# Features times W_a ahead of the aggregation sums, sums in pairs of 64 columns, and 4 KB runs for row 0's second sweep

## Chip, cores and metric

The kernel runs on one core of one Trainium2 chip. The metric is the device time of one execution in microseconds; lower is better. Before the change it is 345.31 us, the median of three runs.

## What is computed

Two graph layers over N = 4096 nodes with D = 64 features, and one dense adjacency matrix `adj` (4096 x 4096, float32, 64 MB, about 1% nonzero):

```python
# layer 0
h = relu(layernorm(x))
for k in range(2):                                  # two hops
    agg = adj @ h
    h = tanh(concatenate([agg, h], axis=1) @ W[k])  # W[k] is 128 x 64
x = x + h
# layer 1
h = relu(layernorm(x))
support = h @ weight                                # 64 x 64
mask = (adj != 0)
rank = cumsum(mask, axis=1); deg = rank[:, -1:]
k = minimum(deg, 100)
pos = rank - (deg - k)
w = mask * where(pos > 0, 0.5 ** (k - pos), 0)
x = x + (w @ support + bias)
```

W[k] has an upper half W_a, for the aggregate, and a lower half W_b, for the node's own features, so a hop is tanh(agg @ W_a + h @ W_b). Layer 1 needs, for each nonzero of a row, how many nonzeros come after it.

## The kernel before

**Tiling.** The adjacency lies transposed in DRAM, cut into 32 blocks of 128 source nodes (`NB`) by 4 "rows" of 1024 target nodes (`NCH`, `CW`). The host's layout, `adjA`, has 16 tiles of 1 MB for each row. A tile of rows 1 to 3 is two blocks by 1024 columns, 8 KB in a run for each partition. A tile of row 0, a "quad", is four blocks by 512 columns. TensorE multiplies features (stationary, 128 nodes by 64 or 128 columns) with the adjacency (moving, 512 columns), so the sums stand transposed in PSUM: features on the partitions, target nodes along the free dimension. Two matmuls with 64 feature columns, one for each half of the 1024 target nodes, go to the two halves of the array's columns (`agg_pair`, L278 to L283): a "pair". A written float32 matmul shows as two recorded instructions.

**Features.** `hxs[q]` holds 8 blocks of nodes with 128 columns: in `[:, :, :D]` the layer norm's output h, in `[:, :, D:]` the features x1 after the first hop, once they are known. `pre1` holds h transposed (`features_T`, L297), later the node's own share h @ W_b (`own_share`, L219), later other things.

**First sweep** (`sweep1`, L464). All four rows go by, 16 tiles each. For every tile TensorE adds h's sums, and VectorE and ScalarE turn the tile into byte codes, which count the nonzeros of each column (`count_tile`, L256). The first step of that, "marking", is done by VectorE (L261), or for chosen tiles ahead of time by ScalarE (`mark_on_act`, L240, two passes of L245 and L246): `marks0` and `MARKS1` list which. When row I is finished, x1 of its 1024 nodes is known, and the later rows take the second hop's sums along for blocks below 8 I ("fused"): there one matmul of 128 columns takes h and x1 together into two banks of `acc[0]` (L606 to L611), and blocks above go in pairs into `acc[1]` (L613). Row 1 has 8 fused blocks, row 2 has 16, row 3 has 24.

**Row end** (`finish_row`, L420; for row 3 `finish_last`, L639). ScalarE copies h's sums from both accumulators into two tiles T and the second hop's share into the lower halves of `xs`; TensorE multiplies T with W_a (`x1_of`, L213, which calls `paired`); VectorE adds the own share; ScalarE takes tanh. Some tiles later `x1_and_share` (L340) transposes x1 back to nodes and multiplies with the second hop's W_b in the same matmuls, and the results are copied away (`take`, L354). These generators go on a list of `steps`, advanced once for each tile. Row 0 has its own end in two halves (`finish_first`, L358). After a row, `set_after` and then `settle` (L452) subtract the totals from that row's codes, 16 times in the first sweep, at odd tiles of rows 2 and 3.

**Buffers and queues.** Tiles are loaded from SP's queue in order, into 5 ring buffers of 1 MB and into areas where codes are not yet needed. A load waits on SP until every reader of the buffer is done, and all loads behind it wait as well. Temporaries (`tmp`) rotate over 5 buffers.

**Second sweep** (`sweep2`, L930). The 72 blocks that were not fused are loaded again, 512 KB each, and TensorE adds x1's sums with a pair for each (`hop`, L977). A small planner with a clock for each engine (`use`, `pe`) decides while the program is built which comes next: a hop, or a unit of layer 1 (`layer1`, L857), which multiplies weights, decoded from the codes by ScalarE (`convert`, L809) or VectorE (L801, L804), with layer 1's features. The instruction order is fixed by it; it is only a model of the engines. Blocks of rows 2, 3, 2, 1 and 0 come in that order; row 0's 24 blocks are last. For those the load reads, for each partition, two runs of 2 KB (L950 to L952). When a row's last hop is done, `finish_x2` (L678) takes the sums to layer 1's features: copy S, matmul with W_a (L696), sum and tanh y, residual, layer norm. 56 of the 128 units are held back until the hops are done (`n_late`), and the last 32 need row 0's features.

The matmul form of L869, TensorE's layer 1 work, uses float32r and is one recorded instruction of 512 columns. Before the first tile PE does nothing; VectorE makes the first features from x, and `wz`, the weights spread over zeros, is cleared on it (L163).

Of the kernel before, what the change touches and what calls it, by code (L numbers as in the profile page):

```python
# [19 lines left out]
P = 128  # L20
# [24 lines left out]
def gnn_kernel(  # L45
# [113 lines left out]

    warm = spool.tile([P, 1], F32, tag="warm", name="warm")  # L160
    nc.vector.memset(warm, 0.0)
    nc.scalar.activation(warm, warm, AF.Square)
    nc.vector.memset(wz, 0.0)  # L163
# [49 lines left out]
    def x1_of(po, I, terms, xs, sums):  # L213
        paired(po, terms)
        nc.vector.tensor_tensor(sums, po, flat(pre1[:, chunk(I), :]), op=ALU.add)
        for c in range(NC):
            nc.scalar.activation(xs[c][:D], sums[c * D : (c + 1) * D, :], AF.Tanh)

# [139 lines left out]
    def finish_first(acc, quads):  # L358
# [4 lines left out]
        def x1_half(c):  # L363
            S = tmp(name="S")
            nc.scalar.copy(S, low[c])
            yield
            nc.tensor.matmul(po[c * D : (c + 1) * D], w0, S, start=False, stop=True)
            xs[c] = tmp(name="x1T")
            nc.scalar.activation(xs[c][:D], po[c * D : (c + 1) * D], AF.Tanh)
            yield  # L370
            for h in range(2):
                pt = nodes(banks[h])
                for t in range(2):
                    nc.tensor.matmul(
                        pt[:, t, :, c, :], by_t(xs[c])[:D, h, t, :], xw[:D],
                        start=t == 0 and c == 0, stop=True, skip_group_check=True,
                    )
            for h in range(2):
                nc.scalar.copy(
                    as_nodes(hxs[0][:, :, D:])[:, 2 * h : 2 * h + 2, c], nodes(banks[h])[:, :, 0, c]  # L380
                )

        def hop1(b):
            for c in range(NC):
                nc.tensor.matmul(  # L385
                    G[c * D : (c + 1) * D, :], at(b)[:, D:], part_of(quads[c, b // 4], b),
# [33 lines left out]
    def finish_row(I, acc):  # L420
        T = [tmp(name="T") for _ in range(NC)]
        for c in range(NC):
            nc.scalar.copy(T[c][:D], acc[0][:D, c, :])
            nc.scalar.copy(T[c][D:], acc[1][c * D : (c + 1) * D])
        xs = [tmp(name="x1T") for _ in range(NC)]
        for c in range(NC):
            nc.scalar.copy(xs[c][D:], acc[0][D:, c, :])
        both = tmp([P, CW], U8, name="both")
        yield
        x1_of(one(name="po"), I, (lambda c: w0, lambda c: T[c]), xs, T[1])  # L430
# [6 lines left out]
        take(hxs[I][:, :, D:], banks, 0)  # L437
# [26 lines left out]
    def sweep1():  # L464
# [5 lines left out]
        EARLY = 9  # L470
# [33 lines left out]
        def counted(k):  # L504
# [10 lines left out]
        MARKS1 = (5, 7, EARLY, EARLY + 1, 14)  # L515
        marks0 = {1: 3, 3: 5, 7: 7, 9: 11, 11: 13, 13: 15}
        F, S = features_T, own_share
        at_step = {
            1: [(F, 3)], 2: [(S, 3)], 3: [(F, 2)], 4: [(F, 1)], 5: [(F, 0)], 6: [(S, 2)], 8: [(S, 1)],
        }  # L520
        to_count = [*range(8), *range(9, 16), 8]

        for k in range(2 * NQ):
# [29 lines left out]
            for b in (4 * q + n for n in (2, 3, 0, 1)):  # L553
# [6 lines left out]
            order_ = {  # L560
                0: (1, 1, 2), 1: (0, 1, 0), 2: ("n", 0),
            }.get(k, ("n", "n") if k == 7 else ("n",))
# [24 lines left out]
        for k in range(2 * NQ, len(units)):  # L587
# [16 lines left out]
            for r in (1, 0):  # L604
                g = b - 1 + r
                if fused(I, g):  # L606
                    for c in range(NC):
                        nc.tensor.matmul(  # L608
                            acc[0][:, c, :], at(g), a[:, r, c * C : (c + 1) * C],
                            start=g == (3 if I == 1 else CB * I - 1), stop=g == (4 if I == 1 else 0),  # L610
                        )  # L611
                else:
                    agg_pair(acc[1], at(g)[:, :D], a[:, r], g == NB - 1, g == CB * I)  # L613
# [3 lines left out]
            if j % HB in (MARKS1 if j < 2 * HB else (5, 8, 11, 14)):  # L617
                mark(j)
            if I > 1 and n % 2 == 1:
# [19 lines left out]
    def finish_last(acc):  # L639
# [5 lines left out]
        T, xs = ([tmp(name=n) for _ in range(NC)] for n in ("T", "x1T"))  # L645
        for c in range(NC):
            nc.scalar.copy(T[c][:D], acc[0][:D, c, :])
            nc.scalar.copy(T[c][D:], acc[1][c * D : (c + 1) * D])
        for c in range(NC):
            nc.scalar.copy(xs[c][D:], acc[0][D:, c, :])  # L650
        use("ACT", 3.4, 0.2)
        yield
        x1_of(one(name="po"), I, (lambda c: w0, lambda c: T[c]), xs, T[1])
        use("ACT", 1.1, use("DVE", 0.7, use("PE", 0.9) + 0.2) + 0.1)
# [3 lines left out]
        take(hxs[I][:, :, D:], banks, 0)  # L658
# [271 lines left out]
    def sweep2(acc):  # L930
# [14 lines left out]
        def load(k, r, a, t):  # L945
# [31 lines left out]
        def hop(n):  # L977
# [3 lines left out]
            k, r, a, landed = tiles[n]  # L981
            agg_pair(accs[I], at(b)[:, D:], a, (I, b) == firsts[I], (I, b) == lasts[I])
            consumed(k, r, a, pe(0.86, False, landed) + 0.2)
            if n in (1, 3, 5):
                next(last, None)
            if (I, b) in ((0, 2 * CB - 1), (0, 3 * CB - 1)):
                space(place([P, CW], F32R, f"hx{b // CB}", "weights"), clock["PE"] + 0.2)
            for v in ends:
                if v - 10 <= n < v and state["fetch"]:
# [3 lines left out]
            if (I, b) == lasts[I]:  # L993
                gen = finish_x2(I, accs[I])
                chain.append((next(gen), gen))

# [17 lines left out]
        while n < total or state["done"] < len(units) or chain or outs:  # L1014
# [10 lines left out]
            while n + hops < min(total, len(tiles)) and tiles[n + hops][3] <= clock["PE"] + 0.1 + 0.86 * hops:  # L1025
                hops += 1
            if state["wide"]:
# [10 lines left out]
            elif go == 2:  # L1038
                hop(n)
                n += 1  # L1040
            else:
                later = [x[0] for x in chain[:1]]
                if n < total:
                    later.append(tiles[n][3])
# [44 lines left out]
```

## Time and profile before

| | us |
|---|---|
| runs | 344.79, 345.31, 347.46 |
| the profiled execution | 345.83 |
| its span, first to last instruction | 343.2 |
| PE busy / VectorE busy / ScalarE busy / GpSimd busy | 328.2 / 279.9 / 200.9 / 23.6 |
| DMA | 108.44 MB, 316 GB/s over the span |

The stages, from the chain of waits: the first features and cold start to 19.6 us; row 0 to 52.86; row 1 to 96.91; row 2 to 142.78; row 3 to 193.65; hops of rows 3 and 2 to 224; hops of rows 1 and 0 among layer 1's units to 302; the hand-over from the last hop to row 0's features to 316.8; the last 32 units and the output to 343.2.

How to read the views. A group's line gives the line of code, engine, operation, the tiles written and read, shapes and count, then busy time, mean of one, and the idle time just before with what ended it. "PE" is a matmul and "PEld" the load of its stationary operand, which runs beside other matmuls. Shares of busy time are averages: a stage tells what is worth something, not the span. The duration of one matmul contains its way through the array, so the cost of many in a row is read from their starts.

### The profile page before, as it was taken

To read this page: it belongs to the slowest core of one execution; us is meant where nothing else is said; L and a number is where in the kernel's file an instruction comes from. 1 tells how busy PE (TensorE), PEld (TensorE's weight loads), DVE (VectorE), ACT (ScalarE), POOL (GpSimd) and SP (SyncE) were. 2 spreads that over 40 slices of the span, in tenths; PEclk is the share of its full clock that TensorE was granted. 3 is DMA by queue.
4 is the path that set the end of the run, shared out by engine and by line. 5 is a ranking of instruction groups with operands and counts; after the bars stand their busy time and mean duration, and the time that the engine had idled before them with its cause. 6 is when DMAs were issued, how large, how long until landed. Compare 5 with 4: busy or idle time off the path is not lost.

```text
span 343.2 us, 3881 instructions
## 1 busy us (share of the span) xinstructions
PE 328.2 (96%) x1360; PEld 155.2 (45%) x1360; DVE 279.9 (82%) x439; ACT 200.9 (59%) x210; POOL 23.6 (7%) x21
## 2 busy tenths in 40 slices
PE   1899999999999999999999999999999999998995
PEld 0344433333344444344444343343454656367785
DVE  4899999998589999899999395688266799989953
ACT  2296782594466551474342434137378989979980
POOL 2340000000000000000000000422003000003000
PEclk9999999999999999999999999999999999999999
DMA  8999999999999999966988999999998958600012
GB/s 267 420 425 417 420 422 421 421 422 420 422 422 416 379 379 352 356 235 236 376 327 298 298 369 411 395 409 411 406 364 281 333 132 248 203 1 0 2 50 73
DMA packets 25474, 108.44 MB, mean 316 GB/s; under 512 B 2416, under 2 KB 3824, under 8 KB 17392
## 3 DMA queue, kind: packets, MB, share of 16 engines
q1 hardware_dynamic: 25456, 108.21, 82.5%
q8 instruction: 10, 0.16, 0.2%
q14 instruction: 8, 0.07, 0.1%
HBM read 107.15 MB, written 1.05 MB: 315 GB/s over the span
## 4 chain that ended last, share of the span: by engine, by line
PE 81%; DMA 6%; DVE 6%; ACT 3%; issue 3%; SPq 1%; ACTq 0%; POOL 0%; DVEq 0%; POOLq 0%
PE acc L608 24%; PE acc L280 15%; PE acc_low L280 13%; PE accl L869 12%; PE acc L555 4%; DMA ring<-in_adjA_dram 4%; PE acc_low L555 3%; PE po L211 2%; PE pto L917 2%; PE acc L385 2%; ACT weights L809 2%; DMA pre<-in_x_dram 2%; PE pt L348 2%; DVE weights L804 1%; DVE bits L801 1%
## 5 line engine op out<-in xcount | busy, mean ns | idle before, releaser
L809 ACT ACTIVATE weights<-codes 128x1024 fp32r<-128x1024 uint8 x90 | 86.7, 1045 | 12.3 <-PE accl L869 9.7
L608 PE MATMUL acc<-ring,hx 128*128 128x512 f32 x160 | 69.6, 594 | 0.0
L280 PE MATMUL acc<-ring,hx 128*64 128x512 f32 x288 | 66.8, 599 | 0.8 <-DMA ring<-in_adjA_dram 0.8
L869 PE MATMUL accl<-weights,feat 128*128 128x512 f32 x254 | 63.4, 400 | 1.3 <-DVE feat L743 1.0
L869 PEld LDWEIGHTS accl<-weights,feat 128*128 128x128 f32 x254 | 45.9, 188 | 21.2 <-ACT weights L809 6.4
L608 PEld LDWEIGHTS acc<-ring,hx 128*128 128x128 f32 x160 | 30.2, 190 | 39.3 <-issue 38.5
L456 DVE TENSOR_TENSOR codes<-codes,after 128x2048 uint16<-128x2048 uint16 x32 | 38.3, 1219 | 0.1
L280 PEld LDWEIGHTS acc<-ring,hx 128*64 128x64 f32 x288 | 19.3, 136 | 39.8 <-issue 29.8
L261 DVE TENSOR_SCALAR mbuf<-ring 128x2048 uint8<-128x2048 f32 x30 | 36.7, 1222 | 0.1
L246 ACT ACTIVATE codes<-codes 128x2048 uint8<-128x2048 int8 x19 | 36.3, 1910 | 0.6
L254 DVE TENSOR_SCALAR cnt<-codes 128x1024 uint16<-128x1024 uint16 (+1 forms) x80 | 29.9, 373 | 2.7
L804 DVE TENSOR_SCALAR weights<-bits 128x1024 fp32r<-128x1024 f32 x37 | 26.6, 719 | 6.7 <-PE accl L869 3.1
L253 DVE TENSOR_TENSOR codes<-mbuf,cnt 128x1024 uint16<-128x1024 uint16 (+1 forms) x50 | 29.8, 596 | 1.8
L245 ACT ACTIVATE codes<-ring 128x2048 int8<-128x2048 f32 x8 | 15.3, 1913 | 26.5 <-DMA ring<-in_adjA_dram 26.5
L801 DVE TENSOR_SCALAR bits<-codes 128x1024 uint32<-128x1024 uint8 x37 | 25.6, 691 | 0.8
L280 PE MATMUL acc_low<-ring,hx 128*64 128x512 f32 x104 | 25.9, 597 | 0.0
L717 POOL TENSOR_TENSOR pre<-pre,wb 128x512 f32<-128x512 f32 x4 | 5.5, 1380 | 273.5 <-DVE xc L193 273.5
L245 ACT ACTIVATE codes<-codes 128x2048 int8<-128x2048 f32 x11 | 21.0, 1912 | 4.4 <-DMA codes<-in_adjA_dram 4.4
L280 PE MATMUL acc_low<-codes,hx 128*64 128x512 f32 x88 | 21.4, 594 | 0.0
L555 PE MATMUL acc_low<-ring,hx 128*64 128x512 f32 x40 | 13.0, 782 | 8.0 <-DVE hx L201 6.9
L261 DVE TENSOR_SCALAR mbuf<-codes 128x2048 uint8<-128x2048 f32 x15 | 18.3, 1221 | 0.5 <-DMA codes<-in_adjA_dram 0.5
L253 DVE TENSOR_TENSOR codes<-codes,cnt 128x1024 uint16<-128x1024 uint16 (+1 forms) x25 | 14.1, 563 | 5.4 <-ACT codes L246 4.0
(99 smaller groups left out, 282.7 us busy)
## 6 DMA issues: line engine op xcount, KB each, us to landing
ring<-in_adjA_dram SPq DMA_DIRECT2D x74, 512.0 KB, 7.9
ring<-in_adjA_dram SPq DMA_DIRECT2D x37, 1024.0 KB, 8.5
codes<-in_adjA_dram SPq DMA_DIRECT2D x26, 1024.0 KB, 17.8
pre<-in_x_dram SPq DMA_DIRECT2D x4, 256.0 KB, 7.4
xres<-in_x_dram SPq DMA_DIRECT2D x4, 256.0 KB, 7.9
out_dram<-o SPq DMA_DIRECT2D x3, 256.0 KB, 2.6
out_dram<-o SPq DMA_DIRECT2D x2, 128.0 KB, 2.2
wb<-in_weights_dram SPq DMA_DIRECT2D x1, 192.0 KB, 6.5
```

What stands on the lines that cost most here:

```text
L245: nc.scalar.activation(sign, tile_of(I, a), AF.Sign)
L246: nc.scalar.activation(m, sign, AF.Square, scale=float((FLAG - 1 + 0.25) ** 0.5))
L253: nc.vector.tensor_tensor(q, m, cnt, op=ALU.add)
L254: nc.vector.tensor_scalar(cnt, q, 0x7F7F, None, op0=ALU.bitwise_and)
L261: nc.vector.tensor_scalar(m, tile_of(I, a), 0.0, float(FLAG - 1), op0=ALU.not_equal, op1=ALU.mult)
L280: nc.tensor.matmul(acc[c * D : (c + 1) * D, :], src, a[:, c * C : (c + 1) * C], start=first, stop=last,)
L456: nc.vector.tensor_tensor(q, q, a[:, None, :].to_broadcast([P, 4, CW // 2]), op=ALU.subtract)
L555: nc.tensor.matmul(low0[c][h * D : (h + 1) * D, :], at(b)[:, :D], part_of(a, b), start=b >= NB - 2 if c == 0 else k == 8 and b > 1, stop=b ...
L608: nc.tensor.matmul(acc[0][:, c, :], at(g), a[:, r, c * C : (c + 1) * C], start=g == (3 if I == 1 else CB * I - 1), stop=g == (4 if I == 1 ...
L804: nc.vector.tensor_scalar(w, state["bits"].bitcast(F32), 2.0 ** (127 - LOW), None, op0=ALU.mult)
L809: nc.scalar.activation(w, q, AF.Exp, scale=LN2, bias=BIAS)
L869: nc.tensor.matmul(sums[g][:, c, :], feats[J][:, k, :], w[:, c * C : (c + 1) * C], start=first, stop=last,)
```

## The change

The second half of each `hxs` column range is now filled early with h @ W_a (`weighted`), so that the first hop's sums are adj @ (h W_a) and need no product behind them. The halves swap roles when a row ends: x1 is written over h in `[:, :, :D]`, and the hops and `hop1` read `[:, :, :D]`. Row 0's own sums still use h and W_a at the end. Fused blocks take two pairs, one for each half of the features, the second into one bank of `acc[0]`. `row_end` replaces the copies and `x1_of`. Three matmuls of cleared `wz` go first on PE. The lists of what is done at which tile of the first sweep (`at_step`, `order_`, `marks0`, `MARKS1`, `EARLY`, the settles) change: 17 tiles are marked on ScalarE where it was 19, and three of the 16 settles go to row 1. In the second sweep row 0's loads take two blocks by 512 columns, one run of 4 KB, and `hop` uses two such tiles at once, four matmuls, then gives both back; the planner's times for the row end change, and it waits for two tiles in row 0.

```diff
+    nc.vector.memset(wz, 0.0)
+    zeros = wz.rearrange("p c k a e -> p (c k a e)")
+    start = two(name="pw")
+    for _ in range(3):
+        nc.tensor.matmul(start, zeros[:, :P], zeros, start=True, stop=True)
...
-    def x1_of(po, I, terms, xs, sums):
-        paired(po, terms)
-        nc.vector.tensor_tensor(sums, po, flat(pre1[:, chunk(I), :]), op=ALU.add)
+    def row_end(I, acc, sums):
+
+        xs = [tmp(name="x1T") for _ in range(NC)]
+        for c in range(NC):
+            nc.scalar.copy(xs[c][D:], acc[0][c * D : (c + 1) * D, 0, :])
+        nc.vector.tensor_tensor(sums, acc[1], flat(pre1[:, chunk(I), :]), op=ALU.add)
         for c in range(NC):
             nc.scalar.activation(xs[c][:D], sums[c * D : (c + 1) * D, :], AF.Tanh)
+        return xs
+
+    def weighted(I):
+
+        v = by_t(flat(pre1[:, chunk(I), :]))
+        pt = (one if I % 2 else two)(name="pg")
+        for t in range(TC):
+            nc.tensor.matmul(
+                pt[:, t * P : (t + 1) * P].rearrange("p (c e) -> p c e", c=NC),
+                v[:, t // 2, t % 2, :], wz[:, :, 0, 0, :],
+                start=True, stop=True, skip_group_check=True,
+            )
+        nc.scalar.copy(
+            as_nodes(hxs[I][:, :, D:]), pt.rearrange("p (t c e) -> p t c e", t=TC, c=NC)
+        )
...
     def finish_row(I, acc):
-        T = [tmp(name="T") for _ in range(NC)]
-        for c in range(NC):
-            nc.scalar.copy(T[c][:D], acc[0][:D, c, :])
-            nc.scalar.copy(T[c][D:], acc[1][c * D : (c + 1) * D])
-        xs = [tmp(name="x1T") for _ in range(NC)]
-        for c in range(NC):
-            nc.scalar.copy(xs[c][D:], acc[0][D:, c, :])
+        xs = row_end(I, acc, tmp(name="T"))
         both = tmp([P, CW], U8, name="both")
         yield
-        x1_of(one(name="po"), I, (lambda c: w0, lambda c: T[c]), xs, T[1])
         tot = tmp([P, CW], BF16, name="tot")
         totals(I, both, tot)
...
-        EARLY = 9
+        EARLY = 7
...
-        MARKS1 = (5, 7, EARLY, EARLY + 1, 14)
-        marks0 = {1: 3, 3: 5, 7: 7, 9: 11, 11: 13, 13: 15}
-        F, S = features_T, own_share
-        at_step = {
-            1: [(F, 3)], 2: [(S, 3)], 3: [(F, 2)], 4: [(F, 1)], 5: [(F, 0)], 6: [(S, 2)], 8: [(S, 1)],
-        }
+        MARKS1 = (6, 9, 12, 15)
+        marks0 = {1: 2, 2: 4, 7: 8, 10: 13, 11: 15}
+        F, G, S = features_T, weighted, own_share
+        at_step = {1: [(F, 3), (F, 2)], 2: [(G, 3), (G, 2)], 4: [(S, 2)], 5: [(F, 0)], 6: [(G, 0)], 7: [(F, 1)], 8: [(G, 1)], 9: [(S, 3)], 10: [(S, 1)]}
...
-            order_ = {
-                0: (1, 1, 2), 1: (0, 1, 0), 2: ("n", 0),
-            }.get(k, ("n", "n") if k == 7 else ("n",))
+            order_ = {0: (1, 2), 1: (1, 'n', 1), 2: (0,), 3: (0, 0)}.get(k, ("n", "n") if k == 7 else ("n",))
...
+                last = n == HB - 1 and r == 0
+                agg_pair(acc[1], at(g)[:, D:], a[:, r], g == NB - 1, last)
                 if fused(I, g):
-                    for c in range(NC):
-                        nc.tensor.matmul(
-                            acc[0][:, c, :], at(g), a[:, r, c * C : (c + 1) * C],
-                            start=g == (3 if I == 1 else CB * I - 1), stop=g == (4 if I == 1 else 0),
-                        )
-                else:
-                    agg_pair(acc[1], at(g)[:, :D], a[:, r], g == NB - 1, g == CB * I)
+                    agg_pair(
+                        acc[0][:, 0, :], at(g)[:, :D], a[:, r], g == (3 if I == 1 else CB * I - 1), last
+                    )
...
-            if j % HB in (MARKS1 if j < 2 * HB else (5, 8, 11, 14)):
+            if j % HB in (MARKS1 if j < 2 * HB else (7, 10, 11, 12)):
                 mark(j)
-            if I > 1 and n % 2 == 1:
+            if (I, n) in {(1, 6), (1, 10), (1, 15), (2, 1), (2, 5), (2, 7), (2, 9), (2, 11), (2, 13), (2, 15), (3, 1), (3, 3), (3, 5), (3, 7), (3, 9), (3, 13)}:
                 settle()
...
-                v = adjA[0].rearrange("(c q) p r (h i) -> q r h p c i", c=NC, h=2)
-                v = v[b // 4, b // 2 % 2, b % 2]
-                nc.sync.dma_start(a.rearrange("p (c i) -> p c i", c=NC), v)
+                nc.sync.dma_start(a, adjA[0, b % 2 * (NB // 4) + b // 4, :, b // 2 % 2, :])
...
+            if I:
+                agg_pair(accs[I], at(b)[:, :D], tiles[n][2], (I, b) == firsts[I], (I, b) == lasts[I])
+                pe(0.86, False, landed)
+            else:
+                for h in range(2):
+                    for c in range(NC):
+                        nc.tensor.matmul(
+                            accs[0][c * D : (c + 1) * D, :], at(b + h)[:, :D],
+                            tiles[n + c][2][:, h * C : (h + 1) * C],
+                            start=(0, b + h) == firsts[0], stop=(0, b + h) == lasts[0],
+                        )
+                pe(1.72, False, tiles[n + 1][3])
+            size = 1 if I else 2
+            for k, r, a, _ in tiles[n : n + size]:
+                consumed(k, r, a, clock["PE"] + 0.2)
```

`finish_last` changes like `finish_row`: `row_end` comes before its first `yield`, and the `yield` between the copies and the product is gone.

More of the change, by code (lines that the diff above doesn't have):

```diff
@@ L162, in gnn_kernel @@
     nc.scalar.activation(warm, warm, AF.Square)
-    nc.vector.memset(wz, 0.0)
     diff = tmp([P, P], name="diff")
@@ L379, in x1_half @@
                 nc.scalar.copy(
-                    as_nodes(hxs[0][:, :, D:])[:, 2 * h : 2 * h + 2, c], nodes(banks[h])[:, :, 0, c]
+                    as_nodes(hxs[0][:, :, :D])[:, 2 * h : 2 * h + 2, c], nodes(banks[h])[:, :, 0, c]
                 )
@@ L385, in hop1 @@
                 nc.tensor.matmul(
-                    G[c * D : (c + 1) * D, :], at(b)[:, D:], part_of(quads[c, b // 4], b),
+                    G[c * D : (c + 1) * D, :], at(b)[:, :D], part_of(quads[c, b // 4], b),
                     start=b == 3, stop=b == 4,
@@ L436, in finish_row @@
         counts = count_after(I, tot, [acc[0][:, c, :] for c in range(NC)])
-        take(hxs[I][:, :, D:], banks, 0)
+        take(hxs[I][:, :, :D], banks, 0)
         take(pre1[:, chunk(I), :], banks, 1)
@@ L644, in finish_last @@
         totals(I, bytes_[:, :CW], tot)
[L645 to L654, printed above, removed]
+        xs = row_end(I, acc, tmp(name="T"))
+        use("ACT", 1.3, use("DVE", 0.7, use("ACT", 1.3, 0.2)) + 0.1)
         yield
@@ L657, in finish_last @@
         counts = count_after(I, tot, [acc[0][:, c, :] for c in range(NC)])
-        take(hxs[I][:, :, D:], banks, 0)
+        take(hxs[I][:, :, :D], banks, 0)
         take(pre1[:, chunk(I), :], banks, 1)
@@ L980, in hop @@
                 accs[I] = two(name="acc1") if I == 1 else plow.tile([P, C], F32, tag="low", name="acc1")
-            k, r, a, landed = tiles[n]
-            agg_pair(accs[I], at(b)[:, D:], a, (I, b) == firsts[I], (I, b) == lasts[I])
-            consumed(k, r, a, pe(0.86, False, landed) + 0.2)
+            landed = tiles[n][3]
+            if I:
[13 more added lines that the diff above has]
+                consumed(k, r, a, clock["PE"] + 0.2)
             if n in (1, 3, 5):
                 next(last, None)
+            b += size - 1
             if (I, b) in ((0, 2 * CB - 1), (0, 3 * CB - 1)):
@@ L988, in hop @@
             for v in ends:
-                if v - 10 <= n < v and state["fetch"]:
+                if v - 10 <= n + size - 1 < v and state["fetch"]:
                     residual(blocks[v][0])
@@ L995, in hop @@
                 chain.append((next(gen), gen))
+            return size
         def run_chain():
@@ L1026, in sweep2 @@
                 hops += 1
+            if hops == 1 and not blocks[n][0]:
+                hops = 0
             if state["wide"]:
@@ L1038, in sweep2 @@
             elif go == 2:
-                hop(n)
-                n += 1
+                n += hop(n)
             else:
@@ L1043, in sweep2 @@
                 if n < total:
-                    later.append(tiles[n][3])
+                    later.append(tiles[min(n + (not blocks[n][0]), len(tiles) - 1)][3])
                 i = state["done"]
```

## Prediction

> **What bounds the kernel now.** I read the chain of waits first. In it TensorE has 81% of the span, and the biggest terms are matmul lines, all of adjacency times features:
>
> ```profile
> PE 81%; DMA 6%; DVE 6%; ACT 3%; issue 3%; SPq 1%; ACTq 0%; POOL 0%; DVEq 0%; POOLq 0%
> PE acc L608 24%; PE acc L280 15%; PE acc_low L280 13%; PE accl L869 12%; PE acc L555 4%; DMA ring<-in_adjA_dram 4%; PE acc_low L555 3%; PE po L211 2%; PE pto L917 2%; PE acc L385 2%; ACT weights L809 2%; DMA pre<-in_x_dram 2%; PE pt L348 2%; DVE weights L804 1%; DVE bits L801 1%
> ```
>
> Then busy time by stage, with stages cut where the chain changes row. Columns: busy PE, weight loads, VectorE, ScalarE and GpSimd with instruction counts, granted clock, DMA share, GB/s:
>
> ```profile
> 19.60:52.86 33.26, 33.26 (x194) 13.57 (x192) 30.79 (x67) 26.10 (x22) 2.93 (x3) 1.00 1.01 420
> 52.86:96.91 44.05, 44.05 (x174) 16.59 (x170) 38.01 (x58) 24.14 (x22) 0.00 (x0) 1.00 1.01 421
> 96.91:142.78 45.87, 45.87 (x151) 19.35 (x150) 43.82 (x59) 22.06 (x22) 0.00 (x0) 1.00 0.96 382
> 142.78:193.65 50.87, 50.87 (x144) 22.45 (x144) 46.53 (x62) 21.32 (x19) 0.00 (x0) 1.00 0.82 300
> 193.65:224.00 30.35, 29.51 (x140) 11.58 (x142) 19.61 (x25) 11.33 (x19) 3.83 (x2) 1.00 1.00 381
> 224.00:302.00 78.00, 77.82 (x336) 38.01 (x332) 58.50 (x86) 60.60 (x67) 7.15 (x4) 1.00 0.88 302
> ```
>
> The reader is to see that PE is busy for every microsecond of rows 0 to 3 (19.6 to 193.65) and, but for about 1 us, after that until 302. VectorE has 31 to 47 us in these stages, a little under PE. DMA is full to about 110 us, but PE is behind it: in the waits, PE itself waited for a ring tile 0.8 us in all after 200, and that was at 219 to 224. So a microsecond of PE work removed or added in the first sweep is a microsecond, unless a second engine catches up.
>
> Third, the chain in order of time gives PE's prices (start, us, what; a written fp32 matmul is two recorded ones):
>
> ```profile
> 52.86 2.14 PE acc_low L280 x9
> ...
> 113.25 27.66 PE acc L608 x64
> 140.91 1.87 PE acc_low L280 x8
> 142.78 1.23 PE po L211 x3
> ...
> 144.44 3.43 PE acc_low L280 x15
> ```
>
> A pair of 64-column matmuls (x4) costs 0.86 (3.43 / 4 = 0.858); one fused block (x4 of L608) costs 27.66 / 16 = 1.73, which is two pairs. The first stretch of pairs behind a fused one takes 1.87, not 1.72.
>
> **What the Trainium skill says.** (1) "TensorE: Matmul & The Clock Gate", Part 1: an idle TensorE runs at half clock until it has been busy for a window of about 3.4 us, and falls back after an idle window. The trace agrees, from the start of the timeline (start, us, what):
>
> ```profile
> 6.87 3.68 PE L555 MATMUL acc_low<-ring,hx 128*64 128x512 f32 x8 [6.87 <-DVE hx L201]
> ...
> 11.72 3.63 PE L555 MATMUL acc_low<-ring,hx 128*64 128x512 f32 x8 [1.17 <-DMA ring<-in_adjA_dram]
> ...
> 16.05 1.90 PE L555 MATMUL acc_low<-ring,hx 128*64 128x512 f32 x8
> ```
>
> The first two tiles take 3.68 and 3.63 for 8 instructions, the third 1.90. (The granted-clock row reads 1.00 throughout; the durations decide.) (2) "TensorEngine Tiling (Array Packing)", Key Properties: a change of tiling mode drains the array. The trace agrees: 1.87 - 1.72 = 0.15 per change. (3) "DMA: Bandwidth & Descriptors", "Why small descriptors are slow (HBM only)": every packet has a fixed overhead. At 255 to 260 us, with row 0's 2 KB runs, the engines are fully busy at 329 GB/s, against 404 to 413 earlier with 4 KB runs.
>
> **The change part by part.** Negative is a gain.
>
> *Zeros first.* Three fp32 matmuls wait only for wz to be cleared (0.48 us, now first on VectorE, so ready near 1.3) and at half clock take about 3 x 1.71 = 5.1, ending near 6.5; the first real matmul starts at 6.87 when its features are there, so they lie in idle time. If the clock is up by then, tile 1, which cannot start before its data at 11.72, takes 1.90, not 3.63: -1.7. The idle time between tile 0 and tile 1 grows from 1.2 to 2.9 us, under the skill's window. The 0.76 us of waiting before the own share at 18.70 also goes, because that share moves to the ninth step: -0.8. Against this, row 3's and row 2's transposes now sit together after tile 1, and the second waits for features that VectorE writes near 14.5 (its order now puts them ahead of row 1's second sum; 15.68 before). The products that follow wait for ScalarE's two copies of 0.6, queued behind the two copies of the weights: about +0.3. Taken -2.2; bounds -2.5 and, with a cold clock and longer waits, +0.5.
>
> *Features times W_a.* Four times four matmuls of 128 columns. The nearest row is the same form, py of L696: 1.14, plus 0.15 for the mode change, less one change where two stand together: 4 x 1.29 - 0.15 = +5.0. PE is full there, nothing hides them. ScalarE's four copies (0.63 each) replace other copies and find it 26 of 33 us busy.
>
> *Pairs in place of fused columns.* 48 fused blocks cost 7.06 + 7.06 + 27.66 + 41.40 = 83.2; as 96 pairs 96 x 0.858 = 82.4; four changes of mode behind them are 4 x 0.15. Together -1.4. Not shown before is a pair to one bank alternating with a pair to another. The nearest is row 0, where L385 follows L555 in another bank at 0.86 each; bounds -1.4 and +4.
>
> *Row ends.* W_a no longer follows the sums. In row 2, from 142.78 to the next transpose at 147.87 are 5.09, of which 3.43 are the next row's pairs: 1.66 for the two matmuls, because the second waits for ScalarE's copies. Rows 1 and 2: -3.3. The chain is now one copy pair (2 x 0.58) on ScalarE beside one addition (0.69) on VectorE, then two tanh (2 x 0.64): 2.6, beside three tiles (5.2) of the next row, so no wait. Queued behind the addition on VectorE is the next row's counting, and behind that the release of ring tiles; it stands earlier in that queue than before, and VectorE had finished counting row 2 at 140.4, ahead of PE's 142.78. In row 3 only two pairs (1.87) cover the 2.6: 1.65 - 0.8 = -0.85, and then the ring is late next (0.79 us of DMA waits at 219 to 224 already), so -0.5; bounds 0 and -1.65.
>
> *Moved marks and settles.* Two fewer tiles are marked on ScalarE (2 x 3.82 less) and two more on VectorE (2 x 1.22), three of sixteen settles (1.2 each) go from rows 2 and 3 to row 1. Row 1 had 6 us of VectorE time free (38.0 of 44.05, one wait of 3.95), which takes the 6.1 added there with nothing to spare; rows 2 and 3 have 3.7 less. Zero; if the cover fails, VectorE is late at row 1's end by 1 to 2 us, where the 2.6 us of slack hide it. Bounds -0.3 and +2.
>
> *Row 0's 4 KB runs, used in twos.* Each 512 KB tile takes about 1.28 (410 GB/s) and not 1.59 (329). SP's queue issues the same number of loads in the same order, and the residual loads stand at the same places. PE waited for none of these tiles, it had weights to work on. Zero; bounds -1 and +0.3 (the first tile of two is given back 0.86 later).
>
> *The hand-over at the end.* The chain from the last hop, VectorE and PE:
>
> ```profile
> 303.42 0.68 DVE L687 COPY S<-acc 128x512 f32<-128x512 f32 x1
> ...
> 304.16 1.21 PE L696 MATMUL py<-wz,S 128*128 128x128 f32 x8 [0.49 <-DVE S L687]
> ...
> 306.55 0.68 DVE L702 TENSOR_TENSOR y<-py,pre 128x512 f32<-128x512 f32 x1
> ```
>
> The last hop ends at 302.0. The copy S waits on VectorE until 303.42, the sum y until 306.55, both behind conversions and evictions; the features are ready at 316.6 (end of VectorE's L743). In the changed order S is on ScalarE, and that eviction comes before it: up to 1.5 sooner. Two units (2 x 0.465) move ahead of the last hop: up to +0.9. Taken -0.7, bounds -2.5 and +1.
>
> **Sum.** -2.2 + 5.0 - 1.4 - 3.3 - 0.5 - 0.7 = -3.1 (0 for the rest). The profiled execution took 345.83 (span 343.2 and 2.6 around it), 0.5 above the median of 345.31, within the runs' scatter. Forecast **342.7**, 0.8% under the median.
>
> **The rivals.** *A, as summed* (0.55): 342.7, own range 340.5 to 344.8. *B, the tail gives more* (0.20): the hand-over's full -2.5 and row 3's full -1.65 make -6.1, 339.8. For it: ScalarE and VectorE are both full at 280 to 305, so the position of one copy counts. Against it: the 24 units left to do in the hand-over are 11.2 us, and no weights can pass before the features. *C, the zeros do not do what they say* (0.12): the array is cold again, or still, at 11.72, and the start returns -0.3: about 344.6. For it: zeros fill 5.1 us, and a window that doesn't start with them can miss. *D, slower* (0.13): a 64-column pair alternating between two banks, with twice as many weight loads, loses its overlap. Its price is 96 pairs times the excess; it decides from 3.1 / 96 = 0.03 us per pair, and 0.07 makes it 349.4. Against it: weight loads of pairs take 137 ns of about 430, and row 0 alternates at 0.86.
>
> **How the numbers follow.** No change is taken as within 1% (341.9 to 348.8), about what runs between 344.79 and 347.46 can tell. Faster: 0.21 of A and 0.19 of B, 0.40. Slower: 0.08 of D and 0.02 of mishaps in A, 0.10. Same: 0.50. The range 339.0 to 347.0 leaves out most of D and the low end of B.
>
> **What would show it.** Zeros: tile 1 at 11.7 with 1.9, not 3.6. W_a: four groups of 8 at 1.1 before 45 us. Pairs: 0.86 in the fused rows, and 1.72 behind them. Row ends: pairs straight up to the transpose in rows 1 and 2; a gap under 1 us in row 3. So the row ends should come later by about 2.8 at 52.86, by 0.2 at 142.78 and earlier by about 2 at 193.65. 4 KB runs: 400 GB/s after 255 with PE's times unchanged. The forecast is wrong if PE shows waits inside rows 1 to 3, or if the last hop moves by 2 and the end does not.

## The result and the profile after

The change made the kernel slightly faster. The changed kernel takes 343.27 us (median of 21 runs, 341.91 to 345.75) against 345.20 for the kernel before in the same comparison (21 runs); the ratio is 0.9956, 95% interval 0.9938 to 0.9974. It was timed twice more beside the experiments: 0.991 (0.9878 to 0.9943) and 0.9927 (0.9899 to 0.9955). The forecast, 342.7 against 345.31, was a ratio of 0.9924. It lies below the first interval and inside the other two.

The profiled execution of the changed kernel takes 343.04, its span 341.3. Two further profiles of the same kernel, from the repeats, have spans of 341.4 and 340.0. The table shows the effect and how much one execution differs from another (us from the start of the span; "first unit" is the first layer-1 matmul):

| | before | after | repeat 1 | repeat 2 |
|---|---|---|---|---|
| row 0's end on PE | 52.86 | 55.60 | 56.79 | 55.59 |
| row 3's end | 193.65 | 191.85 | 193.04 | 191.84 |
| row 0's end to row 3's end | 140.79 | 136.25 | 136.25 | 136.25 |
| row 3's end to first unit | 31.09 | 31.89 | 30.86 | 30.68 |
| first unit | 224.74 | 223.74 | 223.90 | 222.52 |
| first unit to the end of the span | 118.5 | 117.6 | 117.5 | 117.5 |

The steps that the trace can hold to 0.1 us are the rows (4.5 gained) and the stretch behind the first unit (0.9 gained). The start and the stage before the first unit move by more than a microsecond between executions of one program.

The timeline of the start, of the changed kernel (start, duration, engine, line, operation; in brackets the wait before it and what ended it):

```profile
1.45 5.49 PE L164 MATMUL pw<-wz 128*128 128x512 f32 x6 [1.45 <-DVE warm L166]
6.87 2.04 PE L568 MATMUL acc_low<-ring,hx 128*64 128x512 f32 x8
11.49 1.94 PE L568 MATMUL acc_low<-ring,hx 128*64 128x512 f32 x8 [2.59 <-DMA ring<-in_adjA_dram]
```

Tile 1 (11.49) takes 1.94 where it took 3.63, behind a wait of 2.59. So far this is what the prediction said of the zeros; the experiments say something else.

Busy time by stage of the changed kernel, with stages cut at its own row ends (columns as in the prediction):

```profile
55.60:97.23 41.63, 41.63 (x198) 14.89 (x196) 39.91 (x62) 18.98 (x16) 0.00 (x0) 1.00 1.01 421
97.23:141.10 43.87, 43.87 (x213) 15.78 (x210) 42.60 (x60) 19.83 (x17) 0.00 (x0) 1.00 0.95 385
141.10:191.83 50.73, 50.73 (x244) 18.08 (x242) 43.95 (x61) 20.87 (x18) 0.00 (x0) 1.00 0.86 309
191.83:223.81 31.98, 29.88 (x139) 10.32 (x135) 21.30 (x26) 9.45 (x16) 3.83 (x2) 1.00 1.00 385
```

These stages end where a row's sums end. In the kernel before, the cuts at 96.91 and 142.78 lie two pairs of the next row later: row 1's sums ended at 95.04 and row 2's at 140.91.

```profile
87.98 7.06 PE acc L608 x16
95.04 1.87 PE acc_low L280 x8
```

Cut alike, rows 1, 2 and 3 were 42.18, 45.87 and 52.74 and are 41.63, 43.87 and 50.7. PE is still busy for all of them: no waits, and VectorE at 39.9 to 44.0 has not become the bound. In the stage behind row 3 (191.83 to 223.81), PE is busy for 29.88 of 31.98 and DMA for all of it. The first part of the chain in order of time shows why the rows are shorter, and where row 3 still waits:

```profile
75.77 0.86 PE acc L302 x4
76.63 0.86 PE acc_low L302 x4
...
141.10 5.15 PE acc_low L302 x24
146.25 2.08 PE pt L370 x16
...
191.87 0.58 ACT x1T L221
...
193.72 0.64 ACT x1T L224
194.41 1.92 PE pt L370 x14
```

Pairs to `acc` and `acc_low` alternate at 0.86 each. At the end of row 2 six pairs follow (5.15), then at once the transposes at 146.25: nothing of the old row end is left. In row 3 the chain leaves PE for ScalarE's four operations, 191.87 to 194.36.

The hand-over at the end:

```profile
301.66 0.59 ACT L685 COPY S<-acc 128x512 f32<-128x512 f32 x1 [0.99 <-PE acc L987]
...
315.35 1.86 PE L870 MATMUL accl<-weights,feat 128*128 128x512 f32 x7 [1.54 <-DVE feat L744]
```

The copy S now starts 0.1 after the last hop (301.56) instead of 1.4 after it. The hand-over, from the last hop to row 0's features in use, is 13.8 instead of 14.8; two more units stand ahead of the last hop.

### The profile page after: what moved, and what is told of

Same layout as the page of the kernel before. It is cut to its first block, busy times and chain, and to the rows that moved or that the text cites. A ratio compares the mean times of both kernels' runs of the same rounds, so it can differ in the third digit from the quotient of the medians.

```text
span 341.3 us, 4305 instructions
## 1 busy us (share of the span) xinstructions
PE 329.6 (97%) x1578; PEld 150.1 (44%) x1578; DVE 280.4 (82%) x439; ACT 190.5 (56%) x199; POOL 23.5 (7%) x21
## 3 DMA queue, kind: packets, MB, share of 16 engines
HBM read 107.15 MB, written 1.05 MB: 317 GB/s over the span
## 4 chain that ended last, share of the span: by engine, by line
PE 82%; DMA 12%; DVE 3%; ACT 1%; SPq 0%; issue 0%
PE acc_low L302 25%; PE acc L302 20%; PE accl L870 16%; PE acc L987 6%; DMA codes<-in_adjA_dram 5%; DMA ring<-in_adjA_dram 5%; PE acc L568 4%; PE pto L918 2%; PE acc L407 2%; DMA wb<-in_weights_dram 2%; PE pt L370 2%; PE py L697 1%; PE acc_low L568 1%; PE po L215 1%; PE pg L232 1%; PE pt L396 1%
## 5 line engine op out<-in xcount | busy, mean ns | idle before, releaser
L302 PE MATMUL acc<-ring,hx 128*64 128x512 f32 x352 | 86.3, 597 | 1.7 <-DMA ring<-in_adjA_dram 1.7
L302 PE MATMUL acc_low<-ring,hx 128*64 128x512 f32 x264 | 65.5, 593 | 0.0
L302 PEld LDWEIGHTS acc<-ring,hx 128*64 128x64 f32 x352 | 23.6, 136 | 52.5 <-issue 39.8
L302 PEld LDWEIGHTS acc_low<-ring,hx 128*64 128x64 f32 x264 | 19.0, 137 | 37.5 <-issue 37.4
L267 ACT ACTIVATE codes<-ring 128x2048 int8<-128x2048 f32 x10 | 19.1, 1908 | 27.7 <-DMA ring<-in_adjA_dram 27.6
L283 DVE TENSOR_SCALAR mbuf<-ring 128x2048 uint8<-128x2048 f32 x28 | 34.2, 1221 | 0.0
L268 ACT ACTIVATE codes<-codes 128x2048 uint8<-128x2048 int8 x17 | 32.5, 1910 | 0.5
L302 PE MATMUL acc_low<-codes,hx 128*64 128x512 f32 x120 | 27.8, 593 | 0.0
L987 PE MATMUL acc<-ring,hx 128*64 128x512 f32 x96 | 21.9, 598 | 0.0
L202 POOL TENSOR_TENSOR s<-s,half 128x8 f32<-128x8 f32 (+1 forms) x10 | 16.9, 1688 | 18.2 <-DVE s L201 18.2
L302 PEld LDWEIGHTS acc_low<-codes,hx 128*64 128x64 f32 x120 | 8.5, 137 | 17.0 <-issue 17.0
```

The lines of the kernel that those rows point to most:

```text
L267: nc.scalar.activation(sign, tile_of(I, a), AF.Sign)
L268: nc.scalar.activation(m, sign, AF.Square, scale=float((FLAG - 1 + 0.25) ** 0.5))
L283: nc.vector.tensor_scalar(m, tile_of(I, a), 0.0, float(FLAG - 1), op0=ALU.not_equal, op1=ALU.mult)
L302: nc.tensor.matmul(acc[c * D : (c + 1) * D, :], src, a[:, c * C : (c + 1) * C], start=first, stop=last,)
L987: nc.tensor.matmul(accs[0][c * D : (c + 1) * D, :], at(b + h)[:, :D], tiles[n + c][2][:, h * C : (h + 1) * C], start=(0, b + h) == firsts[ ...
```

## The experiments

The theory at the outset was the prediction's sum; in the first profile its terms up to row 3's end had about the forecast size. The questions were why a lead of 4.9 us in front of row 3's hops (they resume at 196.76 instead of 201.62) left 1.0 at the first unit, and whether the terms that came out right did so for the stated reason. Ratios are to the kernel before on the same chip. Runs e1 to e4 had no run of the changed kernel beside them; the later ones had.

### Without the zeros (e1, e7), and the zeros alone (e10)

e1 leaves out the three products:

```diff
-    zeros = wz.rearrange("p c k a e -> p (c k a e)")
-    start = two(name="pw")
-    for _ in range(3):
-        nc.tensor.matmul(start, zeros[:, :P], zeros, start=True, stop=True)
```

> The changed kernel without the three matmuls on zeros at the start. Theory (first-sweep time is kept, in part): tiles 0 and 1 take about 3.6 us each and not 2.0, the end of row 0 on PE comes 1 to 2 us later than 55.60, and the span grows by 0.5 to 1.5 us over 341.3, because the ring's loads after row 3 take up some of it. Rival (the zeros lie in idle time and tile 1 waits for data anyway): row 0 ends within 0.3 us of 55.60, span within 0.3.

Measured: 342.58 us, ratio 0.9929 (0.9904 to 0.9954); span 339.5, row 0's end at 54.55, 1.05 earlier than with the zeros. In that execution tile 1 had landed when tile 0 was done, and the clock came up in the middle of the two. e7 takes the zeros away as well, and moves row 3's transposes by one hop (next section):

> The changed kernel without its three products of zeros, and with the two transposes of row 3 after the third hop rather than the second. Theory (the zeros bring nothing, the hop's place brings 0.65 by returning ring slots sooner, and the two add up because the first loads of row 1's tiles are then the limit): ratio 0.986 to 0.991, first unit of layer 1 near 222 to 223. Rival (the zeros are worth 1 us or more in most executions, the profiled ones before were lucky): ratio 0.992 to 0.996, with tiles 0 and 1 at 3.6 each in the profile and row 0's end at 56.5 or later.

Measured: 342.10, ratio 0.9922 (0.9892 to 0.9951), against 0.991 (0.9878 to 0.9943) for the changed kernel beside it. The start of e7:

```profile
6.95 3.68 PE L564 MATMUL acc_low<-ring,hx 128*64 128x512 f32 x8 [6.95 <-DVE hx L201]
11.30 1.94 PE L564 MATMUL acc_low<-ring,hx 128*64 128x512 f32 x8 [0.67 <-DMA ring<-in_adjA_dram]
```

Tile 0 is cold, as before the change; tile 1 waits 0.67 and runs at full speed, without any zeros. Row 0's end is at 54.84. Both sides of the expectation fail: there is no gain over the changed kernel beside it, and the two tiles were not both cold. e1 fits neither side either: the theory wanted 0.5 to 1.5 lost and the rival no change within 0.3, and the span is 1.8 shorter.

e10 adds the zeros alone to the kernel before, with `wz` cleared ahead of them:

> The kernel before with only the three products of zeros added and wz cleared first. By the prediction's step: tile 0 and tile 1 at 1.9 to 2.2 instead of 3.7 and 3.6, row 0's end at about 51.2 (52.86 before), and the time 0.3 to 0.6% less. Rival (tile 1 waits for its data and the clock may have fallen back, so the start is won in some executions only, and what is won is waited for elsewhere): row 0's end between 51.5 and 53 and the time within 0.25% of the kernel before.

Measured: 345.41 us, ratio 0.9998 (0.9974 to 1.0023): the zeros alone bring nothing, within 0.9 us. PE and ScalarE at the start of e10:

```profile
7.35 1.94 PE L559 MATMUL acc_low<-ring,hx 128*64 128x512 f32 x8 [0.82 <-DVE hx L205]
...
11.31 1.94 PE L559 MATMUL acc_low<-ring,hx 128*64 128x512 f32 x8 [2.03 <-DMA ring<-in_adjA_dram]
...
17.12 0.63 ACT L198 ACTIVATE sq<-xc 128x512 f32<-128x512 f32 x1 [1.96 <-DVE xc L197]
...
17.66 0.60 ACT L310 COPY pre<-ph 128x512 f32<-128x512 f32 x1
...
18.31 1.08 PE L215 MATMUL po<-pre,wz 128*64 128x512 f32 x4 [1.91 <-ACT pre L310]
```

Here both tiles are warm, 3.4 us less of PE work, and row 0's end is at 52.47, only 0.4 earlier. The own share at 18.31 waits 1.91 instead of 0.76, because its operand is the copy `pre<-ph` on ScalarE at 17.66, which stands behind a layer-norm square that could not start before 17.12. That is what the rival said: the start of the kernel before was bound by the features there, not by PE.

What follows: a warm start is paid back at the next wait in the old order. In the new order tile 1 was warm without zeros in both executions that were profiled, and what the zeros take off tile 0 is waited for at tile 1: 2.59 in the changed kernel and 0.67 in e7, for a tile that starts at 11.49 and at 11.30. No run shows a gain from the zeros.

The clock's side of it shows in the changed kernel and in the other runs that have the zeros. Tile 1 took 1.94 in the changed kernel, e2, e4 and repeat 2, after waits of 2.6 to 2.8; 2.41, 2.66 and 2.82 in e5, repeat 1 and e8, after 2.6 to 2.9; and 3.42 in e3, after 2.67. The first two lines are from repeat 1, the third from e3:

```profile
11.83 2.66 PE L568 MATMUL acc_low<-ring,hx 128*64 128x512 f32 x8 [2.72 <-DMA ring<-in_adjA_dram]
14.21 2.98 PE L324 MATMUL ph<-ident,hx 128*64 128x128 f32 x32
...
11.89 3.42 PE L568 MATMUL acc_low<-ring,hx 128*64 128x512 f32 x8 [2.67 <-DMA ring<-in_adjA_dram]
```

Where the clock falls during tile 1, the transposes behind it are slow too (2.98 in repeat 1, 2.13 in the changed kernel), so e5, repeat 1 and e8 lost as much as e3. From the start of tile 1 to the end of these transposes it is 3.7 in the four executions that keep the clock, 5.2 in these three and 5.0 in e3. In repeat 1 the granted clock is 0.50 from 12.98 to 16.30. A lost clock costs 1.3 to 1.5 here, and row 0 ends at 56.4 to 57.1 instead of 55.6.

How often this happens can be counted, because the record has the mean granted clock of every execution. In the profiles that keep the clock it is 0.997 to 1.000, in those that lose it after the start 0.989 to 0.994. (A cold start is not counted: the kernel before has 1.000 with its two slow tiles.) Executions with 0.995 or less:

| | executions |
|---|---|
| kernel before | 3 of 78 |
| kernel before with zeros (e10) | 5 of 14 |
| changed kernel | 21 of 37 |
| changed kernel without zeros (e1, e7) | 1 of 17 |

In each of the three comparisons of the changed kernel, these executions have a median 1.1 to 1.9 us above that of the others. So on this record the zeros make it more likely that the clock is lost, and they may cost more than they bring. That is a count and not an experiment: the changed kernel with and without its zeros was not run side by side, its variants with the zeros go from 0 of 6 (e2) to 11 of 16 (e8), and where the clock fell is known for the profiled executions only.

The Trainium skill, "TensorE: Matmul & The Clock Gate", Part 1, says that the window of about 3.4 us is free-running, so that it depends on its phase when a kernel's clock changes. The waits above agree: nearly equal waits keep the clock in some executions and lose it in others, and the slow stretch of repeat 1 is 3.3 us long.

### Where the lead before the first unit went (e2, e3, e4, e8)

e2 moves row 3's transposes behind the third hop, so that they never wait for tanh and one ring slot is given back before them:

```diff
-            if n in (1, 3, 5):
+            if n in (2, 4):
```

> The changed kernel, with row 3's transposes of x1 after the third hop of the second sweep and not after the second. Theory (the ring's loads bound the stage to 224 us, and the third hop's ring slot comes back too late because it stands behind transposes that wait for tanh): the 0.36 us of waiting before the transposes goes, the third hop ends 2.5 us earlier, the first unit of layer 1 starts 0.5 to 1.3 us before 223.8, and the span falls by as much. Rival (the loads run at 410 GB/s throughout and nothing in the order of four hops moves them): first unit within 0.2 us of 223.8, span within 0.3 of 341.3.

Measured: 341.10 us, ratio 0.9884 (0.9864 to 0.9904); no wait ahead of the transposes, first unit 0.65 earlier than in the changed kernel. It was run again, beside the changed kernel:

> The changed kernel with row 3's transposes after the third hop, a second time. Theory (the ring's slots come back 0.86 us sooner to the loads that limit the stage from 200 to 224): first unit at 222.9 to 223.3, span 0.5 to 0.8 less than the changed kernel's beside it, time 0.1 to 0.4% less. Rival (the lower time of the first look came from the execution, not from the hop's place): first unit at 223.6 or later and times within 0.1%.

Measured: 343.91, ratio 0.9952 (0.9928 to 0.9976), against 0.9927 (0.9899 to 0.9955) for the changed kernel beside it. The first unit came at 224.41, in an execution that lost the clock at tile 1 and had row 0's end 1.6 later than in e2. The theory's gain is not there. The rival has its first unit, but not its 0.1%: the medians are 0.25% apart, with intervals that overlap. So the lower time of e2 is not shown to be a property of the hop's place. e1 and e7, which differ in that place alone, both have their first unit at 221.94. The same program in two comparisons gave 0.9884 and 0.9952, further apart than either interval. The clock goes with it: none of the six executions of e2 has a mean granted clock of 0.995 or less, but 11 of the 16 of e8. Those 11 have a median of 344.17, the other five 341.83, and e2 341.10.

e3 and e4 add the same 1.72 us of PE work, two pairs into an unused bank, in two places: ahead of the seventh hop of the stage, and in the middle of row 2.

```diff
+            if n == 6:          # e4: if k == 40, in the first sweep
+                pad = two(name="pad")
+                for _ in range(2):
+                    agg_pair(pad, at(b)[:, :D], tiles[n][2], True, True)
```

> The changed kernel with 1.72 us of extra PE work (two pairs into a spare bank, not used) before the seventh hop of the second sweep. Theory (PE is ahead of the ring there): PE's waits for the ring at 211 to 222, 1.7 us in all, shrink by it, the first unit of layer 1 still starts within 0.4 us of 223.8, the span stays within 0.4 of 341.3. Rival (PE is the bound in this stage too): everything behind it moves by 1.7.

> The changed kernel with the same 1.72 us of extra PE work in row 2 of the first sweep. Theory (the slots that start the second sweep's loads come back when PE has used the tiles, so this time is kept): row 3 ends 1.7 later, the first unit of layer 1 starts 1.0 to 1.7 later, and the span is 1.0 to 1.7 longer. Rival (the ring stage or the decoding behind it takes it up like that in the hops): first unit and span within 0.5 us of the changed kernel's.

Measured: e3 341.92, ratio 0.9925 (0.9898 to 0.9953); e4 344.10, ratio 0.9983 (0.9964 to 1.0002), on the same chip. PE's waits for the ring between 193 and 226, in the changed kernel and then in e3 (line, what it waited for, us in total, times, longest):

```profile
PE acc L302 <- DMA ring<-in_adjA_dram: 1.7, 8, 0.3
```

```profile
PE acc L302 <- DMA ring<-in_adjA_dram: 0.5, 1, 0.5
```

With 1.72 more work PE waits 1.2 less, and the first unit stays at 223.8, although row 0 had ended 1.1 later in this execution (the cold tile 1 above). Repeat 1, which ended row 0 as late and has no extra work, has it at 223.9. So in this stage PE runs ahead of the loads, and work put there is mostly hidden. In row 2 less is hidden: row 3's transposes came 1.76 later than in the first profile, but the first unit at 224.45 and the end of the span (342.0) only 0.7 later, between the 1.0 that the theory asked for and the rival's 0.5. The time is above e3's with disjoint intervals, by 0.6% or 2 us, which is more than was added. The lost clock does not explain it: the executions above 0.995 differ as much (341.57 and 343.74). PE work in the rows counts, work in this stage counts little; how much of a microsecond in the rows is kept, the profile and the times do not agree on.

What became of the 4.9 us: two hops of 0.86 were only moved, from ahead of row 3's transposes to behind them, so 3.1 are a real lead. By the first unit the first profile kept 1.0 of it, with 1.7 of waits for the ring. Repeat 2 resumed its hops at 196.74, with the same lead, and kept 2.2, with waits of 1.1; repeat 1 had a lead of 2.0 and kept 0.8. So the ring took about 1 to 2 us of the lead, and how much differs from one execution to the next. The difference between the first profile and repeat 2 begins on SP's queue: the residual load that stands between the last tile of the ring and the next took 1.65 us to issue from 194.70, and 0.55 from 194.34 in repeat 2. From 195 to 200 the DMA moved 301 GB/s in the one and 343 in the other, which at 410 GB/s is 0.5 us of transfer that isn't made up in a stage that is full. What held that issue up is open.

### Row 0's loads (e5)

e5 puts back the loads of two 2 KB runs, single hops, and (not shown) the two conditions by which the planner waits for tiles in twos:

```diff
-                nc.sync.dma_start(a, adjA[0, b % 2 * (NB // 4) + b // 4, :, b // 2 % 2, :])
+                v = adjA[0].rearrange("(c q) p r (h i) -> q r h p c i", c=NC, h=2)
+                v = v[b // 4, b // 2 % 2, b % 2]
+                nc.sync.dma_start(a.rearrange("p (c i) -> p c i", c=NC), v)
...
-            size = 1 if I else 2
+            size = 1
```

> The changed kernel with row 0's second-sweep loads as before: 2 KB runs, each tile used by itself. Theory (the 4 KB runs were hidden, PE had weights to work on): DMA share of 1.00 at about 329 GB/s in 255 to 260 comes back, PE has no wait there, and the time is within 0.3% of the changed kernel (under 1 us). Rival (they carry part of the gain: the ring's slots come back to the last hops earlier): slower by 1 us or more, with PE waits for a ring tile between 255 and 302.

Measured: 343.84, ratio 0.9969 (0.9946 to 0.9992), against 0.991 (0.9878 to 0.9943) beside it: the change without its 4 KB runs, used in twos, is 0.6% slower. From the first unit to the end of the span it takes 118.8; the eleven other profiles with the changed second sweep have 117.2 to 117.6. From 255 to 260 the DMA share is 0.96 at 335 GB/s, and 0.81 at 324 in the changed kernel. The stretch before the last hop of e5, and then of the changed kernel:

```profile
289.06 7.95 PE L302 MATMUL acc<-ring,hx 128*64 128x512 f32 x36
297.88 1.08 PE L302 MATMUL acc<-ring,hx 128*64 128x512 f32 x4 [0.87 <-DMA ring<-in_adjA_dram]
298.89 2.14 PE L870 MATMUL accl<-weights,feat 128*128 128x512 f32 x8
300.95 1.94 PE L302 MATMUL acc<-ring,hx 128*64 128x512 f32 x8
```

```profile
286.97 5.78 PE L870 MATMUL accl<-weights,feat 128*128 128x512 f32 x24
292.67 8.95 PE L987 MATMUL acc<-ring,hx 128*64 128x512 f32 x40
301.56 1.20 PE L870 MATMUL accl<-weights,feat 128*128 128x512 f32 x4
```

In e5 the ring is late for the hop at 297.88 (0.87), and the hops behind 255 come in seven stretches between units; in the changed kernel they come in five, the last of them ten pairs long. The last hop ends 79.4 after the first unit instead of 77.8. Of these 1.55, 0.87 is the wait; two stretches more are four changes between hops and units, 0.6 as an estimate from the prediction's 0.15 each. The hand-over behind it is 0.3 shorter, which leaves 1.2. The theory fails. The lower DMA share alone was no measure of it: PE waited for none of these tiles in the kernel before, but the changed kernel's PE with the old loads does. The shorter runs and the other order of hops were put back together, so their shares are not separated.

### The lists of the first sweep (e6, e9)

e6 takes all lists of the first sweep from the kernel before (`EARLY`, `MARKS1`, `marks0`, `order_`, the settles, and `at_step` with each new product one step after its features):

> The changed kernel with the lists of the kernel before: which row-0 and first-sweep tiles are marked early and on ScalarE, when settles come, and at which step of row 0 features, own shares (and with them the new products) are made. Theory (moved marks and settles are worth nothing, the own share's wait of 0.76 comes back): row 0's end 0.5 to 1 later than the changed kernel's 55.6, no PE waits of more than 0.3 in rows 1 to 3, time within 1 us of the changed kernel. Rival (the lists are what keeps VectorE and ScalarE in step with the shortened rows): PE waits at the ends of rows 1 to 3 or before the transposes of 1 to 3 us in sum, and the time 1.5 us or more above the changed kernel's, above the kernel before's or near it.

Measured: 348.87, ratio 1.011 (1.0077 to 1.0142), row 0's end at 63.43. The loss is in row 0, where neither side put it; in rows 1 to 3 PE has no wait with the old lists either. e9 keeps the new lists but for the steps:

```diff
-        at_step = {1: [(F, 3), (F, 2)], 2: [(G, 3), (G, 2)], 4: [(S, 2)], 5: [(F, 0)], 6: [(G, 0)], 7: [(F, 1)], 8: [(G, 1)], 9: [(S, 3)], 10: [(S, 1)]}
+        at_step = {1: [(F, 3)], 2: [(G, 3), (S, 3)], 3: [(F, 2)], 4: [(G, 2), (F, 1)], 5: [(G, 1), (F, 0)], 6: [(G, 0), (S, 2)], 8: [(S, 1)]}
```

> The changed kernel with only the steps of row 0 as before (features of row 3, 2, 1, 0, the own shares at steps 2, 6 and 8, each product after its features); marks, settles and VectorE's order stay as changed. Theory (with all the old lists PE lost 6.6 us in row 0 because ScalarE's copies of the new products queue behind a mark of 3.8 us that the old list puts there): without the old marks most of it goes, row 0's end at 56.5 to 58.5, time 0 to 0.6% above the changed kernel's. Rival (the loss came from the steps, product and own share asked for too soon after the features): row 0's end at 61 or later and the time 1% or more above it.

Measured: 348.44, ratio 1.0081 (1.0046 to 1.0116), row 0's end at 63.34: the rival holds, and the steps alone make nearly all of it. PE in row 0 of e9:

```profile
20.76 1.09 PE L324 MATMUL ph<-ident,hx 128*64 128x128 f32 x16 [0.98 <-ACT hx L237]
...
25.51 1.25 PE L232 MATMUL pg<-wz,pre 128*128 128x128 f32 x8 [1.94 <-ACT pre L328]
27.43 1.97 PE L324 MATMUL ph<-ident,hx 128*64 128x128 f32 x16 [0.68 <-ACT hx L237]
29.20 3.62 PE L568 MATMUL acc_low<-codes,hx 128*64 128x512 f32 x8
...
34.90 1.09 PE L324 MATMUL ph<-ident,hx 128*64 128x128 f32 x16 [0.67 <-ACT hx L237]
```

Each of these blocks of transposes (`ph`) goes to the PSUM bank that an earlier product (`pg`) filled, since two banks alternate for such short results, and waits for ScalarE's copy of that product (`hx`, L237); each product close behind its transposes waits for their copy (`pre`, L328; 1.94 behind a mark on ScalarE). So a mark in the way, which the theory had in mind, is part of it, though it is one of the new list. That is 4.3 us on these lines. After two waits of 1.94 and 0.68 in 4 us the clock is down again: the transposes at 27.43 take 1.97 instead of 1.09 and the tile at 29.20 takes 3.62, with a granted clock of 0.50 from 27.5 to 33. With the waits and the slow stretch row 0 ends 7.7 later than in repeat 2, and the span is 7.6 longer: this loss goes through the ring's stage undiminished.

## Why the prediction was right, point by point

- **Zeros first, -2.2.** This is the step that failed, although its sign in the trace was as said. The 1.7 for tile 1 rested on a warm clock bought by zeros that must outlast a wait "under the skill's window". Neither half is assured: with the zeros the clock was lost at tile 1 in e3, e5, e8 and repeat 1, and tile 1 was warm without them in e7. The wait ahead of tile 1, which the prediction itself put at 2.9 with the zeros, is where these four lost it, and the low clock is in 21 of 37 executions with the zeros and 1 of 17 without. In the order before, e10 shows that a warm start is waited away at the own share. Row 0 ended earlier without the zeros (54.55 and 54.84) than with them (55.6), so in these profiles the gain did not need them. The 0.8 for the own share is real: there is no wait there in the three profiles of the changed kernel, because it moved to later steps.
- **Features times W_a, +5.0.** Four groups of 2.08 together for the first two, 1.14 and 1.14, and three drains of 0.15 make 4.8. Row 0's end was said to come 2.8 later and came 2.7, 3.9 and 2.7 later. What the step did not say is that it holds for these steps only: with the old ones it costs 7.7 more (e9).
- **Pairs -1.4 and row ends -3.3.** -4.7 was said for rows 1 to 3 with row 0's end as zero; 140.79 became 136.25, so -4.5 in each of the three profiles: about -0.5, -2.0 and -2.0 by row, with the cuts of both kernels at the ends of the sums. Row 2's sums end 0.2 later and row 3's 1.8 earlier than before, as said. No run took the products, the pairs and the row ends apart; their sizes are read from PE's times in stages without waits. Rival D, alternating pairs at 0.93, is refuted by 0.86.
- **Row 3's end, -0.5.** From row 3's end to the first unit it was +0.8, -0.2 and -0.4. The gap ahead of the transposes was 0.4 and not the 0.8 that was said, and the ring is late behind it, as said. What the ring takes, put at 0.35, was 1 to 2 us, and varied by more than the term.
- **Moved marks and settles, 0.** No wait in rows 1 to 3, so the free time of VectorE was enough; with the old marks and settles (e6) there is none either. Not tried: the settles alone.
- **4 KB runs, 0.** Failed in size: about -1.2 (e5), outside the bounds of -1 and +0.3. The argument that PE waited for none of these tiles was taken from the order of the kernel before; in the changed order the same loads, used singly, make PE wait and split the hops further. The sign that was named, 400 GB/s after 255, did not come as a rate (324 from 255 to 260), because the engines were busy for only 0.81 of that time.
- **Hand-over, -0.7.** S moved 1.3 closer to the hop and the hand-over is 1.0 shorter. From the first unit on, the last hop ends 0.55 later (two units moved ahead of it, 0.9), the hand-over gives -1.0 and the last units -0.5, together -0.9. In e5, without the 4 KB runs, the hand-over and the last units give as much (-1.3 and -0.5), but the last hop ends 2.1 later, in all +0.3. So the hand-over did what was said of it, and the 4 KB runs used in twos keep the new order from losing that gain ahead of the last hop.

The sum of -3.1 stands against -1.9, -1.8 and -3.2 in the spans of the three profiles. That the total held is partly luck: the credit given to the zeros was there in PE's time at tile 1, whoever earned it, and the loads, put at nothing, kept a gain that stood in for what the ring took. Whether the kernel before usually has a cold tile 1 is open; there is one profile of it.

## What to carry to other kernels

A wait ended by a DMA landing or by another engine's copy takes back what is gained ahead of it: to price a faster start, look at which wait comes next, not only at the instructions that get shorter. A product that is moved to an earlier, busier stage costs only its own time if it can be copied out before the next user of its bank comes; the list of steps is then part of the change and has to be priced with it. And when kernels differ by under 1%, run the control beside each, and compare the granted clocks too, since single profiles of one program differed by 1.4 us here and one ratio did not repeat within its interval.

## What was not expected of the hardware

Single waits of 2.59 to 2.76 us left TensorE its full clock in four executions, and waits of 2.55 to 2.86 lost it in four others, for 1.3 to 1.5 us each; the slow stretch can begin a microsecond after the wait has ended (repeat 1: tile 1 starts at 11.83, half clock at 12.98). In the middle of row 0 it was lost after two waits of 1.94 and 0.68 us within 4 us (e9: a tile of 3.62 instead of 1.89) and after one of 2.09 (e6: 3.52). Pairs that alternate between two banks cost the same 0.86 as pairs to one.
